# Four-head attention units with fp32 scores on 32-row tiles in the grouped-query layer of a cross-attention stack

## The chip, the cores and the metric

The kernel runs on one core of a Trainium2 chip. The core has a matmul engine (TensorE, PE in the profile; its weight loads are listed apart as PEld), VectorE (DVE), ScalarE (ACT), GpSimd (POOL) and SyncE (SP, which here only issues DMAs). The engines run side by side and wait for one another through semaphores. The metric is the device time of one launch in microseconds (us), a median over several executions. Beside it stands one profiled execution, from which all durations below are taken.

## What is computed

Four cross-attention layers run one after the other on x (2048 rows of 256) against a context of 1601 rows of 512. Layers 0, 2 and 3 have 16 heads of 64 and a per-row penalty on a few chosen context columns (the masked layers). Layer 1 is the one that the change is about: it normalizes x first, and its 16 query heads of 16 elements share 4 key/value heads (the grouped layer).

```python
# layer 1
inv = rsqrt(mean(x * x, axis=-1) + 1e-5);  xn = x * inv * norm_w
q = (xn @ wq).reshape(B, T, 16, 16)
k = (cond @ wk).reshape(B, S, 4, 16)
v = (cond @ wv).reshape(B, S, 4, 16)
qg = q.reshape(B, T, 4, 4, 16)
scores = einsum('btgrd,bsgd->bgrts', qg, k) * 16 ** -0.5
out = einsum('bgrts,bsgd->btgrd', softmax(scores), v)
return x + out @ wo

# layers 0, 2, 3
logits = (x @ Wq) @ (ctx @ Wk).T * 64 ** -0.5 + column penalties
return x + softmax(logits) @ (ctx @ Wv) @ Wo + bo
```

## The kernel before

x is held transposed in SBUF (`xs`: 256 channels on 2 x 128 partitions, 2048 columns). A layer is cut into blocks of heads (`blocks`), a block into units (`units`): a unit is one group of heads on one of four blocks of 512 queries (`QB`). The context is cut into `NT` = 13 chunks of 128 keys (the last has 65). A masked layer has 8 blocks of two heads, so 32 units; the grouped layer has 4 blocks (one for each key/value head) of two pairs (`SUBS`), so 32 units as well: 128 units in all.

The main loop (`for step in range(...)`, L1052) makes one step for each chunk. A step scores chunk `ca` of one unit, exponentiates chunk `cb` of the unit before (17 steps later), and multiplies the values of chunk `cv` (18 steps later). After these it runs small pieces of other work: those that are due at this step (`pieces.at`), and then projections of the next block from a queue, as far as a running credit allows (`Pieces.step`, L978). PE, ACT and DVE run their instructions in the order in which the program writes them; pools of tiles decide which instruction has to wait for a buffer.

The scores of masked units (`masked_scores`, L749) are two fp32 matmuls a step, one for each head, with the contraction on 64 rows; ACT copies them to SBUF, DVE keeps a running maximum (L772), later subtracts the maximum (L837); ACT takes exp (L844); GpSimd adds up the denominators (L849).

Grouped units (L774 to L862) have a contraction of only 16. They split each fp32 number into three bf16 parts and stack the needed products of parts on 128 rows (`split`, `stack`, `Q_PARTS`, `K_PARTS`), so that one bf16 matmul gives fp32-like scores. The scores are computed twice: once with queries on the partitions for the row maxima (`grouped_scores`: two matmuls at L788, one DVE reduction of 128x1024 at L793), and once with keys on the partitions for exp (`exp`: two matmuls at L853 and two 64-row ones at L858, which add the remaining products and the negated maximum, then one ACT exp of 128x1024 at L862). The values (`values`, L865) are two fp32 matmuls a step, whose outputs lie on 64 columns each; a column of ones in `v` gives the denominator.

`denominators` (L884) of a masked unit puts two groups of four transposes and two DVE reductions into the one tile of pool `ps_m`, which all projections, queries and output products use as well (L369, L380, L404, L916). [...] `ps_s` two tiles of two banks, `ps_b` one of two banks, `ps_o` and `ps_m` one bank each. Before layer 1, `normalize` (L654) divides x by its root mean square on DVE and writes the result to DRAM, from where the queries load it.

Of the kernel before, what the change touches and what calls it, by code (L numbers as in the profile page):

```python
# [18 lines left out]
P = 128  # L19
# [14 lines left out]
def tile_cross_attention_stack(ctx: ExitStack, tc: tile.TileContext, t: dict, out: bass.AP):  # L34
# [23 lines left out]

    nc = tc.nc
# [15 lines left out]
    NP = 19  # L75
# [7 lines left out]
    ps_s = ctx.enter_context(tc.tile_pool(name="ps_s", bufs=2, space=PSUM))  # L83
    ps_b = ctx.enter_context(tc.tile_pool(name="ps_b", bufs=1, space=PSUM))
    ps_o = ctx.enter_context(tc.tile_pool(name="ps_o", bufs=1, space=PSUM))
    ps_m = ctx.enter_context(tc.tile_pool(name="ps_m", bufs=1, space=PSUM))

# [3 lines left out]
    nc.vector.memset(ones, 1.0)  # L91

# [117 lines left out]
    def first_context_slice(i):  # L210
# [3 lines left out]
        for c in range(4 * i, min(4 * i + 4, NT)):  # L214
# [6 lines left out]
            pt = ps_s.tile([P, NCT, P], FP, name="s")  # L221
# [14 lines left out]
    MX, RA, RB, RE = 0, 3, 6, 9  # L236
    HALVES = (0, 64)
    max_keys = const.tile([P, P], BF, name="max_keys")
    tail_keys = [const.tile([P, NTAIL], BF, name=f"tail_keys{l}") for l in range(NL)]
    max_cols = const.tile([P, QT, P], FP, name="max_cols")  # L240
# [14 lines left out]
    def token_rows():  # L255
# [6 lines left out]
        nc.gpsimd.memset(max_cols, 0.0)  # L262
# [4 lines left out]
        row_of = small.tile([P, 3], FP, name="row_of", bufs=1)  # L267
        for j, (r0, r1) in enumerate(((MX, RA), (RA, RB), (RB, RE))):
            for h in HALVES:
                nc.vector.tensor_reduce(  # L270
                    row_of[h : h + 64, j : j + 1], ident[h : h + 64, h + r0 : h + r1], AX.X, ALU.add
                )
        for b in range(NB):
            for h in HALVES:
                nc.vector.tensor_copy(
                    max_cols[:, :, h + RA : h + RE],
                    parts[:, :, b * QT : (b + 1) * QT].rearrange("p r q -> p q r"),
                )
            pt = ps_m.tile([P, QT, P], FP, name="pm")
            for q in range(QT):  # L280
                nc.tensor.transpose(pt[:, q, :], max_cols[:, q, :], ident)
            nc.vector.tensor_copy(bias_rows[:, ts(b, QB)], pt.rearrange("p a b -> p (a b)"))
        nc.gpsimd.memset(max_cols, 0.0)
        nc.vector.memset(max_keys, 0.0)
        for h in HALVES:
            nc.vector.memset(max_keys[h : h + RA, :], 1.0)
        for l in range(NL):
# [3 lines left out]
            for to, j in ((0, 0), (1, 2)):  # L291
# [11 lines left out]
            nc.vector.tensor_scalar(tail_keys[l], only, row_of[:, 1:2], row_of[:, 0:1], ALU.mult, ALU.add)  # L303
            nc.vector.scalar_tensor_tensor(
                tail_keys[l], marks[:, 1, :], row_of[:, 2:3], tail_keys[l], ALU.mult, ALU.add
# [13 lines left out]
    den_rows = const.tile([P, 2], FP, name="den_rows")  # L319
    one_row = const.tile([P, 1], FP, name="one_row")  # L320
    nc.gpsimd.memset(one_row, 0.0)
    for h, r in enumerate(HALVES):
        nc.gpsimd.tensor_copy(den_rows[:, h : h + 1], ident[:, r + 16 : r + 17])
        nc.gpsimd.memset(one_row[r : r + RA, :], 1.0)
# [5 lines left out]
    class Masked:  # L330
# [25 lines left out]

        def wo(self, u, sub):
            return u.wo
# [34 lines left out]
        def query_pieces(self, unit):  # L393
# [4 lines left out]
            def queries(j):  # L398
                if j == 0:
                    unit.q = heads.tile([P, QB], FP, name="q")  # L400
# [10 lines left out]
    class Grouped:  # L411
# [3 lines left out]

        BLOCKS, HEADS = 4, 2
        SUBS = [(0, 1), (2, 3)]
        name = "L1_xattn_"
        OWN = 32
        ka = vs = None
        Q_PARTS = (0, 0, 0, 1, 1, 1, 2, 2)  # L430
        K_PARTS = (0, 1, 2, 0, 1, 2, 0, 1)

        def stackers(self, kind, parts):

            both = [const.tile([P, 4, 8, 16], BF, name=f"{kind}{x}") for x in "ab"]
            for x in both:
                nc.gpsimd.memset(x, 0.0)
            for j, part in enumerate(parts):
                half = 0 if part == 0 else 64
                nc.gpsimd.tensor_copy(  # L440
                    both[part // 2][:, :, j, :],
                    ident[:, half : half + 64].rearrange("p (h d) -> p h d", d=16),
                )
            return both

        def load(self, n):
# [3 lines left out]
            if n == 0:  # L450
                self.sel_q = self.stackers("sel_q", self.Q_PARTS)
                self.sel_k = self.stackers("sel_k", self.K_PARTS)
                self.last_q = const.tile([P, 2, P], BF, name="last_q")
                self.last_k = const.tile([P, 4, P], BF, name="last_k")
                nc.gpsimd.memset(self.last_q, 0.0)
                nc.gpsimd.memset(self.last_k, 0.0)
                for h, r in enumerate(HALVES):
                    to = slice(r + self.OWN, r + self.OWN + 16)
                    for i in range(2):
                        j = 64 + 16 * self.SUBS[i][h]  # L460
                        nc.gpsimd.tensor_copy(self.last_q[:, i, to], ident[:, j : j + 16])
                    for g in range(4):
                        j = 64 + 16 * g
                        nc.gpsimd.tensor_copy(self.last_k[:, g, to], ident[:, j : j + 16])
                self.wk = weights.tile([P, NCT, 2, 64], FP, name="wk", bufs=1)
                self.wv = weights.tile([P, NCT, 64], FP, name="wv", bufs=1)
                for half in range(2):
                    nc.sync.dma_start(
                        out=self.wk[:, :, half, :],
                        in_=t[self.name + "wk"].rearrange("(k p) f -> p k f", p=P),  # L470
                    )
                nc.sync.dma_start(
                    out=self.wv, in_=t[self.name + "wv"].rearrange("(k p) f -> p k f", p=P)
                )
            u.wq = weights.tile([P, NC, 2, 64], FP, name="wq")
            for half in range(2):
                nc.sync.dma_start(
                    out=u.wq[:, :, half, :],
                    in_=t[self.name + "wq"][:, ts(n, 64)].rearrange("(k p) f -> p k f", p=P),
                )  # L480
            return u

        def load_wo(self, u):
            u.wo_of = weights.tile([P, 2, C], FP, name="wo")
            nc.gpsimd.memset(u.wo_of, 0.0)
            for i in range(2):
                for h, r in enumerate(HALVES):
                    j = 64 * u.n + 16 * self.SUBS[i][h]
                    nc.sync.dma_start(
                        out=u.wo_of[r : r + 16, i, :], in_=t[self.name + "wo"][j : j + 16, :]  # L490
                    )

        def wo(self, u, sub):
            return u.wo_of[:, sub, :]

        def split(self, src, a, b, scale):

            top = slice(64, P)
            nc.scalar.mul(a, src, scale)
            rest = work.tile([P, 512], FP, name="rest", bufs=1)  # L500
            less = rest[top, : src.shape[1]]
            nc.vector.scalar_tensor_tensor(
                less, src[top], scale, a[top], ALU.mult, ALU.subtract
            )
            nc.vector.tensor_copy(a[top], less)
            nc.vector.tensor_tensor(b[top], less, a[top], ALU.subtract)

        def stack(self, dst, sel, j, a, b):
            n = a.shape[1]
            ps = ps_m.tile([P, 512], FP, name="pm")  # L510
            nc.tensor.matmul(
                ps[:, :n], sel[0][:, j].rearrange("p t d -> p (t d)"), a, start=True, stop=False
            )
            nc.tensor.matmul(
                ps[:, :n], sel[1][64:, j].rearrange("p t d -> p (t d)"), b[64:],
                start=False, stop=True,
            )
            nc.vector.tensor_copy(dst, ps[:, :n])

        def projections(self, u):  # L520
            if u.n:
                return None

            def keys(c, ct):
                if self.ka is None:
                    self.ka = heads.tile([P, T], BF, name="ka", bufs=1)
                    self.kb = heads.tile([P, T], BF, name="kb", bufs=1)
                a, m = TCH[c]
                pk = ps_m.tile([P, QB], FP, name="pm")[:, :m]
                for k in range(NCT):  # L530
                    nc.tensor.matmul(
                        pk, self.wk[:, k].rearrange("p h d -> p (h d)"), ct(k)[:, :m],
                        start=(k == 0), stop=(k == NCT - 1),
                    )
                self.split(pk, self.ka[:, a : a + m], self.kb[:, a : a + m], 1.0)
# [14 lines left out]
        def own_keys(self, u):  # L550


            def begin():
                u.kT = heads.tile([P, T], FP, name="kT")
                both = u.kT[:, :].bitcast(BF)
                u.k8, u.k9 = both[:, :T], both[:, T:]

            def stacked(a, n):
                if u.kT is None:
                    begin()  # L560
                self.stack(
                    u.k8[:, a : a + n], self.sel_k, u.n, self.ka[:, a : a + n],
                    self.kb[:, a : a + n],
                )

            def last(a, n):
                ps = ps_m.tile([P, 512], FP, name="pm")
                nc.tensor.matmul(
                    ps[:, :n], self.last_k[64:, u.n, :], self.kb[64:, a : a + n],
                    start=True, stop=True,  # L570
                )
                nc.scalar.activation(
                    u.k9[:, a : a + n], ps[:, :n], AF.Identity, bias=one_row
# [573 lines left out]
```

## Time and profile before

| | |
|---|---|
| median of three runs | 5645.04 us (5642.35 to 5650.94) |
| the profiled execution, own time | 5638.94 us |
| its span | 5637.2 us |
| PE / DVE / ACT / POOL busy | 93% / 71% / 59% / 54% |
| instructions in the profile | 63697 |

A busy share is the time in which an engine had at least one instruction under way. A matmul row names rows * columns of the stationary operand, then the moving operand (64*128 64x512: 64 rows of contraction, 128 output partitions, 512 columns). An fp32 matmul stands in the profile as two records: L755 is executed 2496 times (96 masked units, 13 chunks, two heads) and has 4992 records. A line of the timeline merges neighbouring records of one line of code; its second number lasts to the modelled end of the last of them, and the next group may start before that end, so the distance between starts is what a group costs.

### The profile page before, as it was taken

What the parts mean: (1) busy time and instruction counts of PE and PEld (TensorE: products, weight loads), DVE (VectorE), ACT (ScalarE), POOL (GpSimd) and SP (SyncE); (2) the same over time, 40 slices, a digit from 0 to 9 for tenths busy, and PEclk for the clock granted to TensorE, in tenths of its full rate; (3) what the DMA queues carried; (4) which work ended last, traced back from release to release, by engine and by line L of the source; (5) the groups of instructions that cost most, each with busy time, mean ns of one, the idle gap of its engine ahead of it and who ended that gap; (6) DMA issues with size and microseconds to landing.
All of it is one profiled execution on the core that took longest, in us unless ns stands there. A gap on an engine that the chain in (4) does not pass through costs nothing.

```text
span 5637.2 us, 63697 instructions
## 1 busy us (share of the span) xinstructions
PE 5255.5 (93%) x23412; PEld 2070.8 (37%) x23412; DVE 3981.3 (71%) x4183; ACT 3346.0 (59%) x4096; POOL 3018.6 (54%) x1476
## 2 busy tenths in 40 slices
PE   6899999998889999999999999999999999999997
PEld 4333433343322333233334334333334333334332
DVE  3777777778765555555557777777777777777786
ACT  2666666665533333333356667666667666667675
POOL 1677777775520000000026777777777777777777
PEclk8999999999889999999999999999999999999998
DMA  4222222222100000001112222222222222222211
GB/s 122 63 68 82 75 69 79 76 72 57 53 29 11 16 15 15 11 17 27 47 47 76 78 74 75 78 73 74 78 72 75 77 75 71 77 73 77 74 37 33
DMA packets 341864, 337.99 MB, mean 60 GB/s; under 512 B 110089, under 2 KB 295689, under 8 KB 341552
## 3 DMA queue, kind: packets, MB, share of 16 engines
q1 hardware_dynamic: 338288, 328.53, 20.6%
q8 instruction: 185, 3.03, 0.2%
q0 software_dynamic: 1152, 3.28, 0.2%
q10 hardware_dynamic: 2112, 2.10, 0.1%
q14 instruction: 127, 1.04, 0.1%
HBM read 319.16 MB, written 14.68 MB: 59 GB/s over the span
## 4 chain that ended last, share of the span: by engine, by line
PE 80%; DVE 9%; ACT 7%; issue 3%; DMA 1%; POOL 0%; SPq 0%; ACTq 0%; POOLq 0%; DVEq 0%; another core or an unknown queue 0%
PE po L872 24%; PE s L755 20%; PE pm L369 6%; PE pm L380 6%; PE pm L916 4%; PE pm L404 4%; ACT p L767 3%; DVE p L837 2%; PE s L853 2%; PE s L788 2%; PE s L809 2%; ACT p L844 2%; PE s L858 2%; DVE top L772 2%; PE pm L892 1%
## 5 line engine op out<-in xcount | busy, mean ns | idle before, releaser
L849 POOL TENSOR_TENSOR sums<-sums,p 128x1024 f32<-128x1024 f32 (+1 forms) x1152 | 2725.1, 2366 | 1089.6 <-ACT p L844 1012.1
L872 PE MATMUL po<-p,v 128*64 128x512 f32 (+1 forms) x6656 | 1813.3, 624 | 83.8 <-ACT p L844 44.3
L767 ACT COPY p<-s 128x1024 f32<-128x1024 f32 (+1 forms) x1248 | 1262.3, 1012 | 951.5 <-PE s L755 787.0
L772 DVE TENSOR_TENSOR top<-s,top 128x1024 f32<-128x1024 f32 (+1 forms) x1056 | 1291.6, 1223 | 680.4 <-ACT p L767 678.6
L837 DVE TENSOR_TENSOR p<-p,b 128x1024 f32<-128x1024 f32 (+1 forms) x1248 | 1506.5, 1208 | 72.8 <-ACT b L824 71.4
L844 ACT ACTIVATE p<-p 128x1024 f32<-128x1024 f32 (+1 forms) x1248 | 1322.0, 1059 | 169.5 <-DVE p L837 163.3
L755 PE MATMUL s<-q,kT 64*128 64x512 f32 (+1 forms) x4992 | 1414.9, 643 | 5.7 <-DVE top L772 3.6
L910 POOL TENSOR_TENSOR oT<-oT,by 128x512 f32<-128x512 f32 x128 | 163.8, 1280 | 1160.8 <-DMA by<-cols 901.1
L872 PEld LDWEIGHTS po<-p,v 128*64 128x64 f32 (+1 forms) x6656 | 331.5, 135 | 1076.7 <-issue 271.0
L862 ACT ACTIVATE p<-s 128x1024 f32<-128x1024 f32 (+1 forms) x283 | 289.4, 1023 | 439.1 <-PE s L858 439.1
L755 PEld LDWEIGHTS s<-q,kT 64*128 64x128 f32 (+1 forms) x4992 | 368.7, 182 | 450.4 <-issue 223.4
L793 DVE TENSOR_REDUCE row_top<-s 128x2 f32<-128x1024 f32 x261 | 319.0, 1224 | 153.3 <-PE s L788 152.0
L380 PE MATMUL pm<-wv,ct 128*128 128x128 f32 (+1 forms) x2392 | 344.4, 287 | 78.9 <-DVE rden L893 50.7
L380 PEld LDWEIGHTS pm<-wv,ct 128*128 128x128 f32 (+1 forms) x2392 | 286.6, 187 | 284.7 <-issue 142.0
L369 PE MATMUL pm<-ct,wk 128*128 128x128 f32 (+1 forms) x2392 | 346.0, 288 | 45.8 <-DVE rden L893 32.4
L369 PEld LDWEIGHTS pm<-ct,wk 128*128 128x128 f32 x2392 | 290.3, 191 | 258.3 <-issue 175.6
L916 PE MATMUL pm<-oT,wo 128*128 128x512 f32 x512 | 292.2, 653 | 13.3 <-POOL oT L910 12.5
L862 ACT ACTIVATE p<-b 128x1024 f32<-128x1024 f32 (+1 forms) x133 | 136.0, 1023 | 219.4 <-PE b L858 219.4
L922 DVE TENSOR_TENSOR xs<-pm,xs 128x512 f32<-128x512 f32 x232 | 158.3, 682 | 104.3 <-PE pm L916 104.3
L793 DVE TENSOR_REDUCE row_top<-b 128x2 f32<-128x1024 f32 x123 | 150.6, 1224 | 77.5 <-PE b L788 76.7
L383 ACT COPY v<-pm 128x128 f32<-128x128 f32 (+1 forms) x312 | 82.2, 264 | 186.8 <-PE pm L380 179.0
L847 POOL COPY sums<-p 128x1024 f32<-128x1024 f32 x96 | 99.5, 1037 | 170.6 <-ACT p L844 170.6
(187 smaller groups left out, 3451.3 us busy)
## 6 DMA issues: line engine op xcount, KB each, us to landing
ct<-ctxT SPq DMA_DIRECT2D x288, 512.0 KB, 4.0
xT<-xT SPq DMA_DIRECT2D x104, 512.0 KB, 3.5
spread<-cols SPq DMA_DIRECT2D x96, 512.0 KB, 3.7
by<-cols SPq DMA_DIRECT2D x256, 128.0 KB, 3.1
ct<-ctxT SPq DMA_DIRECT2D x48, 130.0 KB, 2.7
wk<-in_L_xattn_Wk_dram SPq DMA_DIRECT2D x24, 256.0 KB, 5.1
wv<-in_L_xattn_Wv_dram SPq DMA_DIRECT2D x24, 256.0 KB, 2.8
xT<-xs SPq DMA_DIRECT2D x12, 512.0 KB, 2.7
```

The source lines that it names most:

```text
L369: nc.tensor.matmul(pk, u.wk[:, k, :], ct(k)[:, :m], start=(k == 0), stop=(k == NCT - 1))
L380: nc.tensor.matmul(pv, ct(k)[:, :m], u.wv[:, k, :], start=(k == 0), stop=(k == NCT - 1))
L755: nc.tensor.matmul(s[:m, h, :], self.u.kT[r, a : a + m], self.q[r, :], start=True, stop=(a != TAIL),)
L767: nc.scalar.copy(p[:m], s[:m])
L772: nc.vector.tensor_tensor(self.top[:m], s[:m], self.top[:m], ALU.max)
L793: nc.vector.tensor_reduce(self.top[:, :, q, k : k + 1], s, AX.X, ALU.max)
L837: nc.vector.tensor_tensor(self.p[c][:m], self.p[c][:m], self.less[:m], ALU.add)
L844: nc.scalar.activation(p[:m], p[:m], AF.Exp)
L849: nc.gpsimd.tensor_tensor(self.sums[:m], self.sums[:m], p[:m], ALU.add)
L862: nc.scalar.activation(p[:m], s[:m], AF.Exp)
L872: nc.tensor.matmul(self.po[r, :], u.v[:m, c, r], self.p[c][:m, h, :], start=(c == 0), stop=(c == NT - 1),)
L916: nc.tensor.matmul(py, wo[:, ts(k, P)], self.oT, start=True, stop=True)
```

## The change

Only the grouped layer's attention is rewritten; the masked layers change in their denominators.

- A grouped unit has four heads (`SUBS = [(0, 1, 2, 3)]`), so there are 16 such units in place of 32. Queries and keys stay fp32: head h has its 16 elements on rows 32h to 32h+15 (`QUARTERS`), row 32h+16 holds a one for the keys and the negated maximum for the queries.
- A step has two parts. In each, two heads have their maxima scored (`row_maxima`) and the other two their exp scores (`scores_again`), alternately, each an fp32 matmul on 32 rows of its own with 512 columns; then DVE reduces two tiles of 128x512, ACT exponentiates two tiles of 128x512, and the values of the chunk before are multiplied for half of the queries: four fp32 matmuls, each on 32 columns of its own, with 256 moving columns.
- While only grouped work is in the pipeline, `ps_s` and `ps_b` give way to six tiles of one bank (`ps_t`); at the two ends of the layer, pairs of banks are used as before.
- The bf16 splitting, stacking, `max_cols` and `max_rows` are gone. The maxima go through DRAM into the queries' row 16.
- The normalization is no longer applied to x: `norm_factors` computes one factor for each row, spreads it over the partitions through DRAM, and DVE multiplies the queries by it as it moves them out of PSUM; `norm_w` is multiplied into `wq` on GpSimd.
- `denominators` of a masked unit transposes both heads in one piece into a tile of `ps_s` (8 transposes, one DVE reduction of 128x1024), two steps after the last values, in place of one head one step after and the other two steps after in `ps_m`.
- Pools: `probs` has 21 buffers (19), `q` three (two).

```diff
+        def singly(self):
+            scores_pools.close()
+            self.pairs = self.third = None
+            self.banks = scores_pools.enter_context(tc.tile_pool(name="ps_t", bufs=6, space=PSUM))
+        def heads(self, three):
+            if self.banks:
+                return [self.banks.tile([P, 1, QB], FP, name="t") for _ in range(2)]
+            self.turn += 1
+            return [self.b() if three and self.turn % 3 == 0 else self.pair()]
...
-        BLOCKS, HEADS = 4, 2
-        SUBS = [(0, 1), (2, 3)]
+        BLOCKS = 4
+        SUBS = [(0, 1, 2, 3)]
...
-                    self.split(pq, u.qab[:, 0, part], u.qab[:, 1, part], 16 ** -0.5)
+                nc.vector.tensor_tensor(unit.q[:, part], pq, factors[:, unit.b, part], ALU.mult)
...
+        def row_maxima(self, i, h, s):
...
+            for q, a, n, at in todo:
+                nc.tensor.matmul(
+                    s[:, at : at + n], self.q[r, columns(q)], self.u.kT[r, a : a + n],
+                    start=True, stop=True,
+                )
+        def scores_again(self, c, h, s):
             a, m = TCH[c]
+            r = self.rows(h, 17)
+            nc.tensor.matmul(
+                s[:m], self.u.kT[r, a : a + m], self.q[r, :], start=True, stop=True
+            )
...
+                    at = ts(part, QB // 2)
+                    to, v = self.po[r, at], u.v[:m, c, :]
+                    p = self.p[c][h // 2][:m, h % 2, at]
...
-                pt = ps_m.tile([P, QT, P], FP, name="pm")
-                for q in range(QT):
-                    nc.tensor.transpose(pt[:, q, :], self.sums[:, h, columns(q)], ident)
-                nc.vector.tensor_reduce(rden[:, h, :], pt, AX.X, ALU.add)
+                for pt in psum.heads(False):
+                    of = range(h, h + pt.shape[1])
+                    pt = pt.rearrange("p h (q k) -> p h q k", k=P)
+                    for h in of:
+                        for q in range(QT):
+                            nc.tensor.transpose(
+                                pt[:, h - of[0], q, :], self.sums[:, h, columns(q)], ident
+                            )
+                    h += 1
+                    nc.vector.tensor_reduce(rden[:, of[0] : h, :], pt, AX.X, ALU.add)
...
+        for part in range(2):
+            tops = psum.heads(three) if scoring and not scoring.masked else []
+            exps = psum.heads(three) if exping and not exping.masked else []
+            of_tops, of_exps = 2 * (1 - part), 2 * part
...
+            for j in range(2):
+                if tops:
+                    scoring.row_maxima(ca, of_tops + j, bank(tops, j))
+                if exps:
+                    exping.scores_again(cb, of_exps + j, bank(exps, j))
+            for j, tile_ in enumerate(tops):
+                scoring.row_maximum(ca, of_tops + j, tile_)
+            for j, tile_ in enumerate(exps):
+                exping.grouped_exp(cb, of_exps + j, tile_)
+            if valuing and not valuing.masked:
+                valuing.values(cv, part)
```

## The prediction, on record before the changed kernel ran

> **What bounds the kernel now.** I read the page's busy times and chain first, then windows by stage, then the timeline of PE, then PE's groups.
>
> ```profile
> PE 5255.5 (93%) x23412; PEld 2070.8 (37%) x23412; DVE 3981.3 (71%) x4183; ACT 3346.0 (59%) x4096; POOL 3018.6 (54%) x1476
> ...
> PE 80%; DVE 9%; ACT 7%; issue 3%; DMA 1%; POOL 0%; SPq 0%; ACTq 0%; POOLq 0%; DVEq 0%; another core or an unknown queue 0%
> ...
> 1517.00:2894.00 1377.00, 1277.39 (x5527) 426.59 (x5523) 765.66 (x1070) 528.58 (x592) 89.57 (x74) 0.98 0.08 23
> 3000.00:5000.00 2000.00, 1929.53 (x8770) 795.00 (x8771) 1553.19 (x1457) 1382.65 (x1718) 1437.93 (x658) 1.00 0.27 75
> 1290.00:1517.00 227.00, 190.02 (x772) 76.08 (x771) 178.56 (x190) 125.17 (x157) 125.84 (x65) 0.89 0.19 52
> ```
>
> The window columns are length, busy of PE, PEld, DVE, ACT and POOL, granted clock, DMA. PE is the bound everywhere. Where the stages lie is read from the one reduction that each unit makes of its maxima (L810 masked, L816 grouped; first and last start):
>
> ```profile
> L810 DVE TENSOR_REDUCE ntop<-s x5: 1215/1224/1226, 1290.6 to 1516.7; 128x8 f32<-128x1024 f32 x5
> ...
> L816 DVE TENSOR_REDUCE ntop<-row_top x32: 174/176/177, 1564.3 to 2841.9; 128x8 f32<-128x32 f32 x32
> ...
> L810 DVE TENSOR_REDUCE ntop<-s x60: 1224/1225/1226, 2894.2 to 5415.6; 128x8 f32<-128x1024 f32 x60
> ```
>
> From 1517 to 2894, 1377 us, stand 32 grouped units and one masked one, 41.7 us each. A masked unit takes 42 us ((5415.6 - 2894.2) / 60). The last four masked units of layer 0 took 226 us, 58 more than 4 x 42. Now PE's timeline in a masked and in a grouped stretch:
>
> ```profile
> 3202.11 1.13 PE L916 MATMUL pm<-oT,wo 128*128 128x512 f32 x2
> ...
> 3205.20 1.13 PE L755 MATMUL s<-q,kT 64*128 64x512 f32 x4
> 3206.26 1.23 PE L809 MATMUL s<-ident,top 128*128 128x128 f32 x8
> 3207.41 1.08 PE L872 MATMUL po<-p,v 128*64 128x512 f32 x4
> 3208.42 1.13 PE L755 MATMUL s<-q,kT 64*128 64x512 f32 x4
> ...
> 1703.16 0.60 PE L788 MATMUL s<-kT,q 128*128 128x512 bf16 x2
> 1703.61 0.59 PE L853 MATMUL s<-q,kT 128*128 128x512 bf16 x2
> 1704.13 0.39 PE L858 MATMUL s<-max_rows,kT 64*128 64x512 bf16 x2
> 1704.45 1.08 PE L872 MATMUL po<-p,v 128*64 128x512 f32 x4
> 1705.47 0.60 PE L788 MATMUL b<-kT,q 128*128 128x512 bf16 x2
> ```
>
> One full fp32 matmul of 512 columns (L916) and two fp32 matmuls side by side on 64 rows (L755) both take 1.13 us, 1.06 from start to start (3205.20 to 3206.26); two on 64 columns (L872) take 1.01. So two tiles run for the price of one. A grouped step takes 2.31 us (1703.16 to 1705.47), of which the values are 1.01; 13 steps are 30.0 of the 41 us, the rest are pieces and their stalls.
>
> [...] The trace shows tiles of two only, without loss: the four records of L755 at 3205 all start within 0.5 us, two and two, although a pass alone streams for 0.43. Four at a time, no row of before shows; [...]
>
> **The change part by part.**
>
> *A part of a grouped step, PE.* Four score matmuls, if all four rows run together, cost one wave: 1.06, and I add 0.04 for four starts. The values: 256 columns in place of 512. The queries (L611, 48 records, 13.6 us busy from 1900 to 2400) give 0.57 for an fp32 matmul of 256 columns against 1.06 for one of 512, so 256 columns less save 0.49; 1.01 becomes about 0.55. A part is 1.65, a step of two parts 3.30, for four heads. Today four heads are two steps, 4.62. The bounds for what isn't shown: row tiles two at a time, +0.86 a part (two more passes of 0.43, the distance at which the pairs of L755's records start at 123.96, 124.39 and 124.81, where two masked steps follow with nothing between); column tiles two at a time, +0.43 (the same for half the columns).
>
> *DVE, ACT and the banks.* DVE reduces four tiles of 128x512, 0.68 each (L893, same shape: 0.681), 2.7 us a step; ACT does four exps at about 0.59 (L878, a copy of that shape, 0.585; exp and copy of 1024 differ by 11 ns), 2.3. Both are under 3.3. But their banks matter: by the order of release the six banks fall into three for maxima and three for exps, so the second maxima matmul of a part waits for the first reduction of the part before. That is ready at 1.13 (matmul) + 0.04 (start of DVE after PE, L788 to L793) + 0.68 + 0.06 (start of PE after DVE, L893 to L369) = 1.91 after that part began; PE wants it at 1.65. Stall 0.26. Everything behind it on PE is 0.26 late, so in the next part the wait is over (3.56 against 3.56). It recurs in every second part: a step is 3.56. What queues behind the waiting matmul are the second exp matmul and all the values.
>
> *The rest of a unit on PE.* Four query matmuls 2.27, denominators 2.0 (L900: 24.3 us for 96 records, eight a unit), two output matmuls 2.25 (L916), spreading the next keys 0.9 (3.5 us a block, a quarter each), waits for the pool `pm` 1.6 as now (20 us from 1900 to 2400, 12 units): 9.0. Stacking, `last`, and the transposes of maxima go. A unit is 13 x 3.56 + 9.0 = 55.3; two units today 82.
>
> *The ends of the layer.* In the first grouped unit, maxima run beside the masked subtraction: DVE 1.21 + 2 x 1.22 = 3.65 a step and some 4.5 of pieces, 52 us. In the last, exps run beside masked scores: PE 1.06 + 2 x (1.06 + 0.55) = 4.28 a step and pieces, 65. So 1377 becomes 52 + 15 x 55.3 + 65 = 946: **-431**.
>
> *Before the layer.* Key splitting (L505 alone 19 us on DVE from 1290 to 1700) and the division of x (L675 15 us, L677 18) go. Of the 58 us I take 35 off (15 to 55: the low clock there, 0.89, may stay). The factors' matmuls have 16 records at 0.25 instead of two matmuls of 512: +2 us four times. **-27.** The factors' round trip through DRAM (a `by` load lands in 3.1 us) has eleven steps until the queries need it, and the maxima's (one write, four reads) has four steps, 14 us, for some 9; on SP nothing long stands before them.
>
> *Masked denominators.* PE stands idle for them today:
>
> ```profile
>   PE pm L380: 50.7, 40
> ...
>   PE pm L369: 32.4, 24
> ```
>
> These and smaller ones are 86 us, as the projections wait for the reduction to free `pm`: 0.90 a unit. One group of eight transposes (1.15 start to start, L809) in place of two of four (0.67 each) saves 0.19. New: the next scores need the other `s` tile, which DVE releases 3.49 us after its scores began (L755 at 3237.49, L772 ends at 3240.98), while PE arrives after 1.06 + 1.01 + 1.16 = 3.23: a stall of 0.32 with the hand-over. 96 x 0.77 = **-74** (20 to 100).
>
> Pools of 21 and three buffers, POOL's scaling of `wq` and a simpler `v` are not on PE's path: 0.
>
> *Sum.* 5638.94 - 431 - 27 - 74 = 5107 for the profiled execution, which lay 6 under the median of the runs: **5113**.
>
> **Rivals.**
> 1. Columns only two at a time. The four values matmuls each stream all 128 rows; nothing in before shows four. A part is 2.08, over the 1.91, so the stall goes: step 4.16, +0.60 x 13 x 16 = +125: 5240.
> 2. Rows only two at a time[...] (each matmul has two passes). Part 2.51, step 5.02: +1.46 x 208 = +304: 5417. With rival 1 as well, 5.88: 5596. Against it: the pairs now show no such loss.
> 3. Slower: the row tiles run one after the other, each 0.86, since the waits on banks between the four matmuls let no two overlap. A part is 4 x 0.86 + 0.2 + 0.55 = 4.19, a step 8.4: +4.8 x 208 = +1000: 6110. It is slower than before once a step passes 3.56 + 532/208 = 6.1, four score matmuls over 2.5 us. Against it: only one of the four should wait, and for 0.26.
>
> **How the numbers follow.** Forecast 0.65, with its own range 5010 to 5210 [...]; rival 1 0.14; rival 2 alone 0.11, with rival 1 0.04; rival 3 0.06. The range takes in the forecast, rivals 1 and 2: 5005 to 5430. Within 0.2% (11 us, about what a measurement of this kernel can tell from no change) lies none of the cases, only the gap between rival 2 with 1 and rival 3: 0.01, taken from the former. Slower is rival 3, 0.06; faster the rest, 0.93.
>
> **What would show it.** Right: grouped reductions of maxima 55 us apart; four score matmuls in a wave of 1.1 us, four values in 0.55; idle PE before the second maxima matmul of every second part with a DVE reduction as releaser; masked units 41.2 us apart and no PE idle behind the denominators' reduction. Wrong: score waves of 1.9 us or more, value groups of 1.0, or exps that wait for the maxima's DMA.

## The result and the profile after

The changed kernel takes 5565.89 us (median of four runs, 5557.05 to 5575.01) where the kernel before, run beside it, takes 5644.07: a ratio of 0.9859, interval 0.9841 to 0.9877. It is 78 us faster; 532 were forecast, and the time lies outside the range. The profiled execution took 5566.19 us, with a span of 5564.5.

The page of the kernel after gives PE even more of the span than before, and its row of granted TensorE clocks has a hole:

```profile
PE 5377.6 (97%) x25652; PEld 2179.5 (39%) x25652; DVE 3759.2 (68%) x3887; ACT 3329.0 (60%) x4398; POOL 2996.1 (54%) x1429
...
PEclk9999999999665565666789999999999999999998
```

Each digit stands for a fortieth of the span, about 139 us. The same row of the kernel before has only a dip to 8 at the start of that stage:

```profile
PEclk8999999999889999999999999999999999999998
```

Digits 11 to 21, from 1390 us on, are the grouped layer. The windows of the kernel after put numbers on it (length, busy of PE, PEld, DVE, ACT and POOL, granted clock, DMA):

```profile
1600.00:1700.00 100.00, 100.00 (x494) 31.51 (x494) 37.84 (x62) 32.02 (x59) 2.76 (x4) 0.50 0.05 10
1900.00:2000.00 100.00, 100.00 (x580) 37.44 (x580) 44.67 (x75) 36.19 (x68) 3.07 (x5) 0.65 0.07 16
2100.00:2200.00 100.00, 100.00 (x548) 34.16 (x548) 42.31 (x70) 34.86 (x64) 1.26 (x1) 0.59 0.03 9
3000.00:5000.00 2000.00, 1963.50 (x8950) 807.99 (x8948) 1583.04 (x1441) 1411.93 (x1756) 1474.12 (x673) 1.00 0.27 77
```

In the first three windows, all in the grouped stage, PE is busy without a gap (100.00 of 100.00 us), and yet it is granted 0.5 to 0.65 of its clock; in the masked stage after it, the clock is 1.00. "Busy 100%" here is an engine at half speed. The records of the clock in this trace hold two values only, 0.5 and 1.0, so a mean is a share of time: over the whole grouped stage it is 0.63, which is half speed for about three quarters of it.

What one grouped part looks like at half speed, from PE's timeline of the kernel after (start, time to the modelled end, line, shape, records):

```profile
2014.03 1.24 PE L698 MATMUL t<-kT,q 16*128 16x512 f32 x1
2014.03 1.22 PE L762 MATMUL t<-q,kT 17*128 17x512 f32 x1
2014.04 1.23 PE L698 MATMUL t<-kT,q 16*128 16x512 f32 x1
2014.05 2.06 PE L762 MATMUL t<-q,kT 17*128 17x512 f32 x2
...
2016.06 1.08 PE L791 MATMUL po<-p,v 128*32 128x256 f32 x8
2017.07 1.24 PE L698 MATMUL t<-kT,q 16*128 16x512 f32 x1
```

All four row tiles start within 0.02 us: four rows do run at once. But the wave lasts 2.03 us (2014.03 to 2016.06), the values 1.01, the part 3.04, a step of two such parts 6.1. Some 60 us later the same kernel has its full clock for a while. It comes back just behind query matmuls (L557), which use the whole array (128*128):

```profile
2067.30 2.08 PE L557 MATMUL pm<-xT,wq 128*128 128x256 f32 x4
2069.31 0.88 PE L698 MATMUL t<-kT,q 16*128 16x512 f32 x1
...
2074.20 0.81 PE L698 MATMUL t<-kT,q 16*128 16x512 f32 x1
...
2075.39 0.64 PE L791 MATMUL po<-p,v 128*32 128x256 f32 x8
2075.96 0.81 PE L698 MATMUL t<-kT,q 16*128 16x512 f32 x1
2075.96 0.69 PE L762 MATMUL t<-q,kT 17*128 17x512 f32 x1
2076.23 0.81 PE L698 MATMUL t<-kT,q 16*128 16x512 f32 x1
...
2077.40 0.64 PE L791 MATMUL po<-p,v 128*32 128x256 f32 x8
2077.97 0.81 PE L698 MATMUL t<-kT,q 16*128 16x512 f32 x1
```

There the wave of four score matmuls is 1.19 us (2074.20 to 2075.39), the values 0.57, the second maxima matmul of the next part comes 0.27 after the first (2075.96, 2076.23), and a step is 3.77 (2074.20 to 2077.97). The one reduction of maxima in each unit (L733 grouped, L727 masked; first and last start) gives the lengths:

```profile
L727 DVE TENSOR_REDUCE ntop<-s x96: 1212/1225/1226, 128.4 to 5494.1; 128x8 f32<-128x1024 f32 x96
L733 DVE TENSOR_REDUCE ntop<-row_top x16: 207/209/214, 1500.6 to 2781.0; 128x16 f32<-128x64 f32 x16
```

A grouped unit takes (2781.0 - 1500.6) / 15 = 85.4 us. The difference of the two spans, cut at the masked reductions of each trace, is:

| stretch | before | after | difference |
|---|---|---|---|
| start to the first masked maxima | 140.4 | 128.4 | -12 |
| 27 masked units | 1150.2 | 1130.3 | -20 |
| the last four of layer 0 | 226.1 | 172.8 | -53 |
| grouped stage, to the first maxima of layer 2 | 1377.4 | 1436.9 | **+60** |
| the next three units | 142.5 | 148.7 | +6 |
| 56 masked units (42.48 and 41.60 each) | 2378.9 | 2329.7 | -49 |
| the rest | 221.6 | 217.7 | -4 |
| span | 5637.2 | 5564.5 | -73 |

So everything that the change gained, it gained outside the attention that it rewrites. The first line is not its doing: in the runs below that stretch takes between 128 and 139 us, and 130.3 in the one with the new denominators alone, whose work up to there is that of the kernel before.

### The profile page after: what moved, and what is told of

It reads as the page before. It is cut to its first block, busy times and chain, and to the rows that moved or that the text cites. A ratio compares the mean times of both kernels' runs of the same rounds, so it can differ in the third digit from the quotient of the medians.

```text
span 5564.5 us, 67946 instructions
## 1 busy us (share of the span) xinstructions
PE 5377.6 (97%) x25652; PEld 2179.5 (39%) x25652; DVE 3759.2 (68%) x3887; ACT 3329.0 (60%) x4398; POOL 2996.1 (54%) x1429
## 4 chain that ended last, share of the span: by engine, by line
PE 84%; ACT 8%; DVE 6%; issue 1%; DMA 1%; POOL 0%; ACTq 0%; SPq 0%; POOLq 0%; DVEq 0%
PE po L791 24%; PE s L668 21%; PE t L698 8%; PE pm L415 6%; PE pm L404 6%; PE t L762 5%; ACT p L680 4%; PE pm L837 4%; PE pm L439 4%; DVE top L685 3%; ACT p L752 2%; PE s L726 2%; DVE p L747 1%; PE pm L557 1%; PE pm L821 1%
## 5 line engine op out<-in xcount | busy, mean ns | idle before, releaser
L791 PE MATMUL po<-p,v 128*64 128x512 f32 (+3 forms) x8320 | 1748.2, 593 | 45.5 <-ACT oT L796 22.5
L791 PEld LDWEIGHTS po<-p,v 128*64 128x64 f32 (+3 forms) x8320 | 327.3, 133 | 1411.3 <-issue 702.6
L773 ACT ACTIVATE p<-t 128x512 f32<-128x512 f32 (+1 forms) x764 | 418.6, 595 | 760.8 <-PE t L698 686.3
L710 DVE TENSOR_REDUCE row_top<-t 128x1 f32<-128x512 f32 x704 | 453.7, 686 | 523.4 <-PE t L698 520.8
L832 POOL TENSOR_TENSOR oT<-oT,by 128x512 f32<-128x512 f32 x112 | 142.8, 1275 | 1130.3 <-DMA by<-cols 997.5
L698 PE MATMUL t<-kT,q 16*128 16x512 f32 (+1 forms) x1888 | 745.7, 846 | 0.0
L762 PE MATMUL t<-q,kT 17*128 17x512 f32 (+1 forms) x1528 | 715.6, 960 | 0.0
L698 PEld LDWEIGHTS t<-kT,q 16*128 16x128 f32 x1888 | 298.8, 316 | 253.2 <-DVE row_top L710 162.8
L837 PE MATMUL pm<-oT,wo 128*128 128x512 f32 x448 | 275.3, 699 | 11.2 <-POOL oT L832 10.3
L762 PEld LDWEIGHTS t<-q,kT 17*128 17x128 f32 (+1 forms) x1528 | 193.3, 259 | 0.0
```

The costliest lines, as they stand in the source:

```text
L698: nc.tensor.matmul(s[:, at : at + n], self.q[r, columns(q)], self.u.kT[r, a : a + n], start=True, stop=True,)
L762: nc.tensor.matmul(s[:m], self.u.kT[r, a : a + m], self.q[r, :], start=True, stop=True)
L791: nc.tensor.matmul(to, v, p, start=(c == 0 and not part), stop=(c == NT - 1 and part != 0))
L837: nc.tensor.matmul(py, self.u.wo[:, ts(k, P)], self.oT, start=True, stop=True)
```

## The experiments

**Which property of the new matmuls lowers the clock.** Theory A: the clock follows the part of the array that is in use, and tiles of 16 or 17 of 32 rows use half of it. Rivals: B, four tiles at once are too great a load; C, the values' 32-column tiles; D, short waits. The edit pads the contraction to all 32 rows of a tile; the added rows add zeros to each sum, and the banks and waits stay as they are. At full clock the two kernels take the same time for a part with a wait in it, 1.44 us up to its values (2075.96 to 2077.40 above, 1743.11 to 1744.55 in the timeline of this run).

```diff
 def row_maxima(self, i, h, s):
-    r = self.rows(h, 16)
+    r = self.rows(h, 32)
...
 def scores_again(self, c, h, s):
-    r = self.rows(h, 17)
+    r = self.rows(h, 32)
```

> Both score matmuls read all 32 rows of their tile (16 and 17 before); the added rows are zero, so the work on every engine stays the same. Theory A (the granted clock follows how many rows of the array a matmul uses; 16 or 17 of 32 is too few): the clock is 1.0 from 1600 to 2600 us, a grouped step takes 3.6 to 3.8 us and the kernel about 5150 us. Theory B (four fp32 tiles at once are too much load): the clock stays near 0.6 or falls, 5560 us or more. Theory C (the values on 32 columns lower the clock) and theory D (PE's short waits in each part lower it): clock near 0.6, about 5566 us.

Measured: 5252.24 us, ratio to the kernel before 0.9305 (0.9289 to 0.9321): two numbers in the code are worth 314 us. Over 800 us in the middle of the grouped stage, the windows of the kernel after and of this one:

```profile
1550.00:2350.00 800.00, 798.44 (x4329) 287.72 (x4328) 328.39 (x542) 278.80 (x506) 17.23 (x26) 0.60 0.05 13
```

```profile
1550.00:2350.00 800.00, 797.73 (x5823) 393.00 (x5824) 437.30 (x722) 370.51 (x681) 21.14 (x29) 0.92 0.07 18
```

The clock goes from 0.60 to 0.92 with PE equally busy, and 1.35 times as many matmuls get through (5823 for 4329). The direction is A's, though not its figures: A expected a clock of 1.0 and about 5150 us. B, C and D fall as causes of the hole, since the four tiles, the values and the waits are all still there. What exactly the clock follows (rows held, operands read) no run separates; it isn't the values in the added rows, which are zeros.

**Only one kind of scores padded, and all to 24 rows.** If what counts is rows in use, and not one of the two sorts of matmul, the halves must share the gain. The next two runs make one of the two edits each, the third puts 24 for both numbers.

> Only the exp scores read 32 rows, the maxima stay at 16. Theory A with a threshold on the mean use: rows in use in a wave rise from 66 to 96 of 128, so either the full gain (about 5150 us) or, if 96 is still under the threshold, little (5450 to 5566); anything between tells that the clock switches more often. Theories B, C and D: about 5566 us.

> Only the maxima read 32 rows, the exp scores stay at 17: 98 of 128 rows in a wave. Theory A: the same as with the exp scores alone, within 50 us. Theories B, C and D: about 5566 us.

> Both kinds of scores on 24 rows instead of 16/17 (after) or 32 (first experiment). If the clock follows rows in use in proportion, the time lies between 5566 and 5252, near 5400, with the clock in the stage near 0.75; if a threshold on the part of the array in use decides, it lies at one end: 5250 to 5290 with a clock above 0.9, or 5520 to 5570 with 0.6.

Measured, one execution each: 5402.83, 5352.86 and 5380.99 us. The same window for exp scores alone, maxima alone, and 24 rows:

```profile
1550.00:2350.00 800.00, 798.44 (x4983) 331.62 (x4985) 378.82 (x626) 320.93 (x586) 19.35 (x28) 0.74 0.06 14
```

```profile
1550.00:2350.00 800.00, 798.44 (x5276) 352.27 (x5272) 400.15 (x661) 337.68 (x616) 19.79 (x28) 0.80 0.06 15
```

```profile
1550.00:2350.00 800.00, 798.44 (x5171) 345.03 (x5170) 394.14 (x650) 332.81 (x607) 20.24 (x29) 0.78 0.06 15
```

| rows of the four tiles, maxima and exp | rows in all | clock | time, us |
|---|---|---|---|
| 16, 17 (after) | 66 | 0.60 | 5566 |
| 16, 32 | 96 | 0.74 | 5403 |
| 24, 24 | 96 | 0.78 | 5381 |
| 32, 17 | 98 | 0.80 | 5353 |
| 32, 32 | 128 | 0.92 | 5252 |

Three ways to have about 96 rows in use give clocks between those of 66 and of 128. Neither sort of matmul is to blame by itself, and the forecast in proportion for 24 rows (near 5400 us, 0.75) comes out. The order of the middle three, one execution each, proves nothing; theory A's forecast for the two halves, the same within 50 us, is met at its very edge.

The mean hides two things, which the records of the clock show beside PE's timeline. In the kernel after, nine of the thirteen falls to half between 1550 and 2600 us begin during the last step of a unit, whose products are short. And all twelve returns to full clock from 1570 to 2590 us come 1.6 to 2.7 us after the start of whole-array matmuls (L557, or the output's L837). Between a return and the next fall the 66 rows run at full clock, for up to 24 us. So it looks as if the rows decide above all how long a fall lasts: up to 147 us with 66 rows, at most 10.2 with 128 (1550 to 2350 us). The short step with only 66 rows was not reordered alone, so what it would give without padding isn't known.

**What is left at 32 rows.** In that run the clock still falls at the end of each unit, at all 13 ends from 1550 to 2350 us. PE's timeline of it, at the end of a unit, where the context's last chunk has 65 keys:

```profile
1746.17 1.38 PE L698 MATMUL t<-kT,q 32*128 32x65 f32 x5
1747.16 0.69 PE L762 MATMUL t<-q,kT 32*128 32x512 f32 x1
...
1749.21 0.82 PE L791 MATMUL po<-p,v 128*32 128x256 f32 x8
1749.96 1.43 PE L698 MATMUL t<-kT,q 32*128 32x65 f32 x5
1750.95 1.22 PE L762 MATMUL t<-q,kT 32*128 32x512 f32 x1
```

The four short maxima products of a head (L698, 65 columns) stand one behind the other on one row tile, with the exp scores behind them; the part takes 3.04 us up to its values (1746.17 to 1749.21), and then L762 needs 1.22 in place of 0.69: half clock. The edit lets the two heads alternate and puts the exp scores first; `row_maxima` takes the block of queries as a last argument and then issues its one product alone:

```diff
 for j in range(2):
-    if tops:
+    if tops and ca < NT - 1:
         scoring.row_maxima(ca, of_tops + j, bank(tops, j))
     if exps:
         exping.scores_again(cb, of_exps + j, bank(exps, j))
+if tops and ca == NT - 1:
+    for q in range(QT):
+        for j in range(2):
+            scoring.row_maxima(ca, of_tops + j, bank(tops, j), q)
```

> Rows of 32 as in the first experiment (5252 us), and the last step of each unit put in another order: the exponentials' scores of both heads are issued first, then the four short maxima products of 65 columns alternating between the two heads, where they stood one head after the other. Theory: in the first experiment's trace such a part took 3.0 us with mostly one row tile in work (1746.17 to 1749.21), and the clock fell to half for 10 us right after it; so if few rows in use over some us is what lowers the clock, the parts become about 1.8 us, the clock drops at unit ends go, and the unit falls from 65.5 to about 59 to 61 us: 5150 to 5190 in all, mean clock 0.98 or more. Rival (the drop has another cause, such as the full-array pieces around the unit end or the time since the clock last rose): only the shorter parts are gained, 2.4 us a unit, 5210, and the windows still show drops once a unit.

Measured: 5187.09 us, ratio 0.9185 (0.917 to 0.92). It is the fastest version here, 379 us under the changed kernel. Its window and its reductions of maxima:

```profile
1550.00:2350.00 800.00, 796.86 (x6278) 397.23 (x6276) 464.24 (x771) 393.50 (x733) 22.37 (x30) 0.97 0.09 23
```

```profile
L733 DVE TENSOR_REDUCE ntop<-row_top x16: 207/209/211, 1500.2 to 2411.7; 128x16 f32<-128x64 f32 x16
```

A unit is (2411.7 - 1500.2) / 15 = 60.8 us, in the middle of the stage 57.7 to 59.3; in the first experiment it was 65.5. The last step of a unit now looks like this:

```profile
1733.57 0.70 PE L762 MATMUL t<-q,kT 32*128 32x512 f32 x2
...
1735.59 0.64 PE L791 MATMUL po<-p,v 128*32 128x256 f32 x8
1736.16 0.70 PE L762 MATMUL t<-q,kT 32*128 32x512 f32 x2
```

Up to its values a part takes 2.02 us (1733.57 to 1735.59) in place of 3.04; 1.8 was expected. Two parts give 2.0 of the 4.7 us by which a unit is shorter, and the rest goes with the clock, which rises from 0.92 to 0.97. So both the theory's gain and the rival's are in the number. Falls are left: from 1500 to 2400 us there are 13, of 3.4 or 6.8 us each. Only three begin at the end of one of the 14 last steps (at 1738 the values again take 1.08 for 0.64). Eight begin within 1.7 us of the start of a unit's last matmul for its denominators:

```profile
1766.82 2.03 PE L821 MATMUL pm<-den_rows,oT 128*128 128x4 f32 x8
1768.78 1.24 PE L698 MATMUL t<-kT,q 32*128 32x512 f32 x1
```

These matmuls have all 128 rows, but only four moving columns each, and the wave behind them runs at half speed (1.24 for 0.81). So the rows of a matmul are not the whole of it: two microseconds in which little streams through the array precede a fall here as well. No run takes L821 away, so this is read from the order in time alone.

**The new denominators alone.** The kernel before, with both heads' sums transposed into one score tile and one reduction, and all else as it was:

```diff
-    pt = ps_m.tile([P, QT, P], FP, name="pm")
-    for q in range(QT):
-        nc.tensor.transpose(pt[:, q, :], self.sums[:, h, columns(q)], ident)
-    nc.vector.tensor_reduce(rden[:, h, :], pt, AX.X, ALU.add)
+    pt = ps_s.tile([P, 2, QB], FP, name="s").rearrange("p h (q k) -> p h q k", k=P)
+    for h in range(2):
+        for q in range(QT):
+            nc.tensor.transpose(pt[:, h, q, :], self.sums[:, h, columns(q)], ident)
+    nc.vector.tensor_reduce(rden, pt, AX.X, ALU.add)
...
-    found = [(1 + h, Piece(lambda h=h: self.denominators(h), 0.5)) for h in range(2)]
+    found = [(2 if self.masked else 1, Piece(self.denominators, 1.0))]
```

> The kernel before with the new denominators of masked units alone (both heads in one piece, two steps after, in the pool of scores). Forecast of the prediction: 0.77 us for each of 96 units, 74 us less, 5570 us. Rival: the wait for the other scores tile gives the gain back, 5630 us or more.

Measured: 5591.49 us, ratio 0.9906 (0.9888 to 0.9924), 53 us gained. PE waits for the reduction no more, as foretold; but a masked unit gains 0.62 us (42.48 to 41.86), where in the changed kernel it gains 0.88. The waits of this run from 3000 to 5000 us show where to look for the difference (sum, times, longest):

```profile
ACT p L767 <- POOL sums L849: 70.3, 70, 3.0
```

```profile
PE po L872 <- ACT p L844: 11.1, 14, 1.8
```

ACT's copy of fresh scores waits for a buffer that GpSimd's sums hold, and PE's values then wait for a late exp. PE's 11.1 us over some 48 units are 0.23 a unit, about the 0.26 in question. In the kernel before ACT's wait is 1.0 us, in the kernel after 5.0:

```profile
ACT p L680 <- POOL sums L757: 5.0, 6, 0.9
```

The change has 21 such buffers where the kernel before, like this run, has 19. The test takes the two away: the fastest version with `NP = 19`.

> The reordered version with 32 rows (5187 us) with 19 buffers for the probabilities in place of 21, the number that the kernel before has. The prediction priced the two buffers at nothing. Theory: in the run with the new denominators alone, which has 19, ACT's copy of the masked scores waits 70 us from 3000 to 5000 for GpSimd's sums to free a buffer (5 us with 21), and PE's values then wait for the exponential 11 us; so the two buffers are what lets the new denominators earn 0.83 a unit instead of 0.5. With 19 the masked units become about 0.3 longer: 25 to 30 us, 5210 to 5220. Rival (the lost part has to do with something else in that kernel, such as the order in which it takes its score tiles): 5187 within 8.

Measured: 5195.00 us (5185.41 to 5208.29), ratio 0.9212 (0.9189 to 0.9234): 8 us more than with 21, far less than the theory's 25 to 30 and at the edge of the rival's, with an interval that overlaps that of 21. Its wait for the buffer is back:

```profile
ACT p L680 <- POOL sums L757: 52.6, 56, 2.1
```

but little of it reaches PE (its values wait 4.9 us for exp, not 11.1): the 56 masked units take 2335.3 us for 2329.6, 0.1 each, and the first one after the grouped stage 60.0 for 52.8. So the two buffers matter little: in these two profiled executions some 12 us in all masked stretches and 7 at that one unit, against a start that happened to be 10 us shorter. Most of the difference between 0.62 and 0.88 is not theirs, and what it is remains open.

## Why the prediction was wrong, step by step

**The bound.** Right: PE bounds the kernel, even at 97%. The sum was right to be made on PE's time.

**A part of a grouped step: the failed step.** Every duration in it was taken from a row at full clock, and the clock of the stage was taken over from the kernel before, 0.98 there with 128 and 64 rows of the array in use. The rivals doubted whether the tiles would overlap; none doubted the clock. The tiles overlap as forecast. What fails is the speed: with 66 of 128 rows in use the clock is half for three quarters of the stage, and a step is 6.1 us for most of the time. That is the very step at which the third rival puts the break-even with the kernel before, and so the stage comes out near its old length, by another mechanism. Two of the signs that the prediction named for being wrong show, waves of 2.03 us and values of 1.01, but they come from the clock and not from lost overlap. Shown: padding alone takes the stage (masked maxima to masked maxima) from 1436.9 to 1127.2 us, -310, and the order of the last step takes it to 1052.0, -75. Together they are 385 of the 491 us by which the stage misses its 946. About 2 us a unit of the second, some 33 in all, are shorter parts and not clock: the sum took 13 equal steps, and the last one, with its short products, is longer (about 7.2 us at full clock as written, twice 3.04 and 0.57; 5.2 reordered; 3.77 for the others).

**The terms of the step.** At full clock: values 0.57 (0.55 forecast), stall of the second maxima matmul 0.27 (0.26), wave 1.19 (1.10), step 3.77 (3.56). The mis-sized term is the wave, 0.09 twice in a step. Over 13 steps the 0.21 make 2.7 us: 55.3 + 2.7 = 58.0, and the middle units of the fastest version take 57.7 to 59.3. So the unit's sum holds in total once the clock is there, in part by luck: the last step is 1.4 longer than the others, and the other work 7.3 to 8.9 us in place of 9.0. The upper end of the prediction's own range, 5210, took a longer wave than the measured 1.19, an estimate of its author. Rivals 1 and 2 are excluded by the waves and the values at full clock, rival 3 by the common start of the four tiles.

**The ends of the layer.** In the fastest version the first grouped unit takes 62.2 us (52 forecast), the last 78.3 (65), and the three before it 63.7 to 69.7: they carry the projections of the next layer's keys and values, which the sum for a unit left out. With the step's 0.21 over the 15 intervals (41 us) these make up 23 + 29 + 41 = 93 of the 106 us that separate 1052.0 from 946. The rest was not separated from what remains of the low clock.

**Before the layer.** -53 instead of -27. Of the 53, about 3.5 belong to the denominators of four units. The forecast took 35 of 58 us off, since the low clock might stay. It did not: PE's waits in those four units, of the kernel before,

```profile
PE po L872 <- ACT p L844: 14.5, 9, 3.1
PE po L872 <- ACT oT L878: 5.3, 2, 4.1
PE pm L568 <- DVE kT L518: 4.3, 3, 2.7
PE pm L543 <- DVE rest L502: 3.7, 1, 3.7
```

have no successors in the kernel after, where its largest waits are

```profile
PE s L668 <- DVE top L685: 1.0, 4, 0.3
PE pm L513 <- DVE xs L841: 1.0, 1, 1.0
```

The clock there goes from 0.89 to 0.97. With splitting and division gone from DVE, the exps no longer come late for the values; that they were what made them late fits the two traces, but is not shown. This part was not run alone; it is read from the two traces.

**Masked denominators.** The prediction's 42 us for a masked unit divides 59 distances by 60. The right mean is 42.7, and 42.48 in the repeating stretch, so that 56 and not 58 us were there to gain before the layer. The gain does not hang on this: 0.88 us a unit in the repeating stretch against 0.77; about 76 us in all (20 + 49 + 4 in the masked stretches, 3.5 before the layer) against 74. The new stall, scores behind DVE's running maximum, is 12.2 us from 3000 to 5000, 0.25 a unit (0.32 forecast). The sum is right; that it needs more than the new reduction is not something that the forecast saw: alone, that reduction is worth 53 us.

**Pools at nothing.** Two more buffers were priced at 0. Taking them away costs 8 us by the medians, at the edge of what can be told.

## What to carry to other kernels

When matmuls use only part of the array's rows, read the granted clock of that stage before the busy share: here PE was busy for 100.00 of 100.00 us at a clock of 0.50, and durations taken from another stage were too short by factors of 1.7 (waves) and 1.8 (values). Where small contractions are packed into row tiles, fill the tiles, with zeros if there is nothing else; here that cost no time and gave 314 us. Look also for short products that stand in line on one tile: spread over the tiles, they gave 65 us more, by their own time and by the clock.

## What the hardware showed that was not expected

- The mean granted clock was lower with fewer rows in use although PE was hardly ever idle (798 of 800 us busy): 0.60, 0.74 to 0.80, 0.92 for 66, 96 to 98 and 128 rows in a wave of four tiles. The rows added from 66 to 128 hold only zeros, and the clock rose with them all the same.
- Four fp32 row tiles of 32 rows run at once for 1.19 us where one matmul takes 1.06, that is 3.6 times the work; four fp32 column tiles of 32 columns show next to no loss, 0.57 us for 256 columns, where one matmul of that width over the whole array takes 0.53 (L557 of the kernel after, two in 1.06 us, 2073.14 to 2074.20).
- A fall to half clock begins mostly where little streams through the array: at a unit's short products (nine of 13 falls with 66 rows, 13 of 13 unit ends with 128) or, with these reordered, at four-column matmuls (eight of 13). How long it lasts goes with the rows of the steps behind it: up to 147 us with 66 rows, where the returns come 1.6 to 2.7 us behind the start of whole-array matmuls, and up to 10.2 us with 128.
